# Routing products on column tiles, and a gate product on both row halves, in a two-layer gated cross-attention kernel

## The chip, the cores and the metric

The kernel is one program on one core of a Trainium2 chip. The metric is device time in microseconds of that core, from one launch that computes all sixteen examples. Lower is better.

## The reference, cut to what matters

The input is x with 16 examples of 256 tokens and 256 features. Two layers follow each other. Each has a gated attention part and a gated feed-forward part. The kernel treats them as four stages:

```python
# stage 0: attention of 16 heads over x and 77 context rows, then x += tanh(g) * (...)
# stage 1: mixture of 8 experts, two per token
logits = x @ router_w.T                       # 256 tokens x 8
probs = softmax(logits); topk_vals, topk_idx = top_k(probs, 2)
out = sum over the two: (x @ expert[topk_idx] + probs[topk_idx]) * topk_vals / (sum + 1e-6)
# stage 2: masked attention of 16 heads onto the context
# stage 3: gated linear attention, 8 heads of 64, 4 experts by token mask
low = xn @ [Wqa | Wka | Wga | Wg1a | We | Wg2a]      # 256 tokens x 256
z = low[:, ga part of 64] @ Wgb                       # 256 tokens x 512, the output gates
o = o * rsqrt(mean(o^2) + eps) * norm_w * silu(z)
x += tanh(g) * (o @ Wo)
```

The change touches two places. One is the routing of stage 1: the logits, and the ranks that say at which row of its expert's list a token goes. The other is z of stage 3, the output gates. Everything is computed in 32-bit floats.

## The kernel before, in words

**Engines and order.** TensorE, VectorE, ScalarE, GpSimd and SyncE (DMA issue) each run a program of their own. The order on an engine is the order in which the code below calls it. `pe`, `dve`, `act`, `pool` and the local `matmul` keep every instruction in that order (the helper at line 50 is the one that the profile names for most of them). An engine waits only where a semaphore makes it. A 32-bit matmul shows as two passes in the profile, so two MATMUL and two LDWEIGHTS records for each call.

**Stage 0** runs over 64 units (example b, head group g of four heads). In a unit TensorE makes the scores of this unit, the values `o` of the unit before it, and the keys and queries `qk` of the next one. The routing of examples already finished is spread over these units. In `behind_values`, `ranks` of example b-2 comes behind the values of g = 2 and `logits` of example b-1 behind those of g = 3. `logits` multiplies with the 256 tokens as the stationary operand (four matmuls of 128x128 against 8 columns). `ranks` multiplies with a triangular matrix `before` and with `ones` as the stationary operand (two matmuls, 16 columns each). Both results are copied out of PSUM by ScalarE in `copied`. The routing of the last two examples falls in stage 1. Early in stage 0, `clear_rows` fills the two lists of routed rows in DRAM with zeros from a tile `zero`, by 16 DMAs on SyncE's queue; the context's values of examples 1 and up pass through DRAM (`vctx`) on the same queue.

**Stage 3** runs over 64 slots p = 4b + m, where m is a pair of heads of example b. The main loop of `stage3_fast` writes the order of a slot out by hand; the tables `start`, `copies`, `middle`, `rest`, `late`, `behind_mask`, `by_rows` and `logs` add the steps that are made once or twice an example. In every slot TensorE makes two score products into one PSUM tile, `products(p, 0)` (`sc<-f` in the profile) and `products(p, 1)` (`sc<-q,k`). The tile `sc` has one buffer, so the second product waits until VectorE has read the first one in `masked(p, 0)` (`at<-sc,amask`). Between the two stand `route_logits`, the output gates and `second` (`gq<-low,lbk` on array rows 0 to 63 and `gz<-low,lbk` on rows 64 to 127). In slots 1 and 2 the values of the slot before (`o<-at,v`) stand there as well; in slots 0 and 3 they come behind `products(p, 1)`.

**The output gates** z of an example are 512 features by 256 tokens, four matmuls with 64 contraction rows, all on array rows 0 to 63 (`zg<-low,lbg`). `outgates(b, 0)` makes two of them in slot 0 and `outgates(b, 1)` the other two in slot 3. ScalarE reads each bank for exp(-z), VectorE copies z out of it (`zs`), ScalarE makes ln(1 + e) and exp(-ln), and GpSimd multiplies the two (`gw`). `gw` is used from slot 3 on.

**PSUM banks.** Steps that need a bank for a moment take it with `bank()`, from a pool of two buffers that are handed out in turn. An example asks for 14 of them in a fixed order. In slot 0 it is: `den` (the key softmax sums), `low`, `rt` (the expert logits of the next example, `route_logits`), `zg`. A bank is written again only when its last reader is through.

Of the kernel before, what the change touches and what calls it, by code (L numbers as in the profile page):

```python
# [10 lines left out]
F32 = mybir.dt.float32  # L11
# [15 lines left out]
def bc(ap, shape, *axes):  # L27

    for a in axes:
        ap = ap.unsqueeze(a)  # L30
    return ap.to_broadcast(list(shape))
# [42 lines left out]
def layers(ctx: ExitStack, tc: tile.TileContext, t, out, check):  # L74
# [66 lines left out]
    wo0 = load_w("wo0h" if fast else "wo0", 1024, D, w0)  # L141
    for b in range(2, B):
        load_x(b)
    rw1 = load_w("rw1", D, 8, ws1)
    ew1 = load_w("ew1", D, 2048, ws1)
    prio = const("prio", [P, 8])
    nc.sync.dma_start(out=prio, in_=t["prio"])
# [1 line left out]
    if fast:  # L149
        bv, own, pmask = (w12.tile(shape, F32, tag=n, name=n) for n, shape in (  # L150
            ("bv", [P, D]), ("own", [P, 2, 32]), ("pmask", [P, 2])))
        before, offs = (ws1.tile(shape, F32, tag=n, name=n) for n, shape in (
            ("before", [P, P]), ("offs", [P, 2, 2, 8])))

        gbo = const("gbo", [P, D])
        for n, x in (("bv", bv), ("bo", gbo), ("own", own), ("pmask", pmask), ("before", before),
                     ("offs", offs)):
            nc.sync.dma_start(out=x, in_=t[n])
    else:
        brow = w12.tile([1, 2, D], F32, tag="brow", name="brow")  # L160
        nc.sync.dma_start(out=brow, in_=t["brow"])
        bmask = w12.tile([P, 4], F32, tag="bmask", name="bmask")
        nc.sync.dma_start(out=bmask, in_=t["bmask"])
# [231 lines left out]
    class Route:  # L395
# [31 lines left out]

        def logits(self, b, bank):
            ps, xnT = bank("rt"), self.xnT.pop(b)
            for i in range(2):  # L430
                for k in range(2):
                    pe.matmul(ps[:, 8 * i:8 * i + 8], xnT[:, k, i * P:(i + 1) * P], rw1[:, k, :],
                              start=k == 0, stop=k == 1)
            self.copied(b, ps[:, :16])

        def copied(self, b, ps):
            n = ps.shape[1]
            self.ps[b] = ws1.tile([P, n], F32, tag=f"copied{n}", name="copied")
            act.copy(self.ps[b], ps)

        def exps(self, b):

            z = self.ps.pop(b)[:, :16].rearrange("p (i e) -> p i e", i=2)
            mx = st.tile([P, 2], F32, tag="rmx", name="rmx")
            dve.tensor_reduce(mx, z, AX.X, ALU.max)
            e = self.e[b] = st.tile([P, 2, 8], F32, tag="re", name="re")
            dve.tensor_tensor(e, z, bc(mx, [P, 2, 8], 2), ALU.subtract)
            act.activation(e, e, AF.Exp)
# [58 lines left out]
        def ranks(self, b, bank):  # L507
            hs, h1, h2 = self.hs[b]
            ps = bank("rank")
            pe.matmul(ps[:, :16], before, hs[:, 0].rearrange("p i e -> p (i e)"), start=True, stop=True)  # L510
            pe.matmul(ps[:, 16:32], ones, hs[:, 1].rearrange("p i e -> p (i e)"), start=True, stop=True)
            self.copied(b, ps[:, :32])

        def place(self, b):

            (_, h1, h2), ps, count = self.hs.pop(b), self.ps.pop(b), check["rows"][:, b // 8]
            base = st.tile([P, 2, 2, 8], F32, tag="base", name="base")
            at = st.tile([P, 2, 2, 2, 8], F32, tag="at", name="at")
            row = st.tile([P, 2, 2, 2], F32, tag="row", name="row")
            n = st.tile([P, 2, 8], F32, tag="nth", name="nth")  # L520
            dve.tensor_tensor(n, ps[:, :16].rearrange("p (i e) -> p i e", i=2), bc(count, [P, 2, 8], 1), ALU.add)
            dve.tensor_tensor(count, count, ps[:, 24:32], ALU.add)
            dve.tensor_tensor(n[:, 1, :], n[:, 1, :], ps[:, 16:24], ALU.add)
            dve.tensor_tensor(base[:, 0], n, offs[:, 0], ALU.add)

            dve.scalar_tensor_tensor(base[:, 1], n, ROWS - 1.0, offs[:, 1], ALU.min, ALU.add)
            for k, h in enumerate((h1, h2)):
                dve.tensor_tensor(at[:, :, :, k], base, bc(h, [P, 2, 2, 8], 1), ALU.mult)
            dve.tensor_reduce(row, at, AX.X, ALU.add)
            dve.tensor_copy(self.pos[:, b], row)  # L530
# [22 lines left out]
        return rows[e * n:e * n + ROWS].rearrange("(p n) d -> p n d", p=P)  # L553

    def clear_rows():
        zero = ws1.tile([P, D], F32, tag="zero", name="zero")
        nc.gpsimd.memset(zero, 0.0)
        n = ROWS // P
        for rows in route.rows:
            for e in range(8):  # L560
                nc.sync.dma_start(out=by_expert(rows, e),
                                  in_=bc(zero, [P, n, D], 1))

    def stage0_fast():
        with ExitStack() as sx:
# [339 lines left out]
    def stage1():  # L905
        with ExitStack() as sx:
# [7 lines left out]
            def route(b):  # L914
# [3 lines left out]
                ps = bank("rt")  # L918
                for i in range(2):
                    for k in range(2):  # L920
                        nc.tensor.matmul(ps[:, 8 * i:8 * i + 8], xnT[:, k, i * P:(i + 1) * P], rw1[:, k, :],
                                         start=k == 0, stop=k == 1)
                shape = [P, 2, 8]
                pr = softmax_last(st, "pr", ps[:, :16].rearrange("p (i e) -> p i e", i=2), shape)
# [692 lines left out]
    def stage3_fast(early_bank):  # L1617

        with ExitStack() as sx:
# [7 lines left out]
            def bank(name):  # L1627
                return pss.tile([P, 512], F32, tag="ps", name=name) if pss else early_bank(name)
# [11 lines left out]
            halves = w1.tile([P, P], F32, tag="halves", name="halves")  # L1640
            nc.sync.dma_start(out=halves, in_=t["halves"])

            lbg2 = w1.tile([64, 512], F32, tag="lbg2", name="lbg2")
            nc.sync.dma_start(out=lbg2, in_=t["lbg"][64:P, :])
            low2 = w1.tile([64, P], F32, tag="low2", name="low2")
            wo = w1.tile([P, 4, D], F32, tag="wo", name="wo")

            hots = [w1.tile([P, 2, 4], F32, tag=f"hot{n}", name=f"hot{n}") for n in range(2)]

            xn, xnT, low, lg, hT, em, am = {}, {}, {}, {}, {}, {}, {}  # L1650
            v, gw, u_, oT = {}, {}, {}, {}


# [32 lines left out]
            def lows(b):  # L1686

                low[b] = of(b).tile([P, 2, S], F32, tag="low", name="low")
                ps = bank("low")
                for c in range(2):  # L1690
                    for k in range(2):
                        matmul(ps[:, c * S:(c + 1) * S], la[:, k, c * P:(c + 1) * P], xnT[b][:, k, :],
                                         start=k == 0, stop=k == 1)
                dve3.tensor_copy(low[b][:, 0, :], ps[:, :S])
                dve3.tensor_scalar(low[b][:, 1, :], ps[:, S:], vec[:, V_ONE:V_ONE + 1], None, ALU.add)
                if b > 0:
                    for r in range(0, 64, 32):
                        dve3.tensor_scalar(low2[r:r + 32, :], ps[64 + r:96 + r, S + P:],
                                           vec[64 + r:96 + r, V_ONE:V_ONE + 1], None, ALU.add)
# [91 lines left out]
                        matmul(ps, xnT[b][:, k, tokens(i)], wv3[:, k, :], start=k == 0, stop=k == 1)  # L1791
                    act3.copy(v[b][:, i, :], ps)

            def outgates(b, i):

                if i == 0:
                    gw[b] = w2.tile([P, 4, S], F32, tag="gw", name="gw")
                ps = bank("zg")
                for m in range(2):
                    matmul(ps[:, m * S:(m + 1) * S], lbg[0:64, (2 * i + m) * P:(2 * i + m + 1) * P],  # L1800
                           low[b][0:64, 1, :], start=True, stop=True)
                e = w2.tile([P, 512], F32, tag="eg", name="eg")
                act3.activation(e, ps, AF.Exp, scale=-1.0)
                z_[b, i] = ps, e

            def outgates_end(b, i):
                ps, e = z_.pop((b, i))
                zs = w2.tile([P, 512], F32, tag="zs", name="zs")
                dve3.tensor_copy(zs, ps)
                act3.activation(e, e, AF.Ln, bias=1.0)  # L1810
                act3.activation(e, e, AF.Exp, scale=-1.0)
                pool3.tensor_tensor(gw[b][:, 2 * i:2 * i + 2, :].rearrange("p m s -> p (m s)"), zs, e, ALU.mult)


            def place(p):
# [168 lines left out]
            def warm():  # L1984

                ps = bank("warm")
                for _ in range(2):
# [7 lines left out]
            rest = {0: [(bias, 2)], 1: [(route, 1)], 2: [(steepest, 1, 0), (stats, 2)], 3: [(steepest, 1, 1), (turn_ahead, 2)]}  # L1995
            late = {1: [(scaled, -1, 1)], 2: [(project, -1)], 3: [(vals, 1)]}
            behind_mask = {0: [(route_logits, 1)]}
            by_rows = {0: [(outgates, 0, 0)], 1: [(gates_end, 1)], 3: [(outgates, 0, 1)]}
            logs = {0: [(route_sums, 1), (outgates_end, 0, 0)], 1: [(gate_logs, 1, 0)], 2: [(gate_logs, 1, 1), (norm_ahead, 2)],
                    3: [(outgates_end, 0, 1)]}  # L2000

            def run(steps, p):
                for f, d, *a in steps.get(p % 4, ()):
# [136 lines left out]
def _arrays(i):  # L2140
# [4 lines left out]
    def cols(v):  # L2145
# [32 lines left out]
        "x": f["x"], "ctx": f["ctx_1024"], "fside": f["fside_BxSxS2_0"], "mask": f["mask_BxSxS2_ik1"], "vec": vec,  # L2178
        "wkv0": f["L0_xattn_Wkv"], "wq0": f["L0_xattn_Wq"], "wo0": f["L0_xattn_Wo"],
        "wo0h": f["L0_xattn_Wo"].reshape(4, 4, 2, 32, D).transpose(0, 2, 1, 3, 4).reshape(1024, D),  # L2180
        "rw1": f["L0_ffn_router_w"].T, "ew1": f["L0_ffn_expert_weights"].transpose(1, 0, 2).reshape(D, 2048),
        "prio": np.broadcast_to(np.arange(8, 0, -1, dtype=np.float32), (P, 8)),
        "wq2": f["L1_xattn_wq_k"], "wk2": f["L1_xattn_wk_k"], "wv2": f["L1_xattn_wv_k"], "wo2": f["L1_xattn_wo_k"],
        "brow": np.stack([f["L1_xattn_wv_b"], f["L1_xattn_wo_b"]])[None], "bmask": bmask.astype(np.float32),
        "la": la, "lbk": lbk, "lbg": lbg, "we3": f["L1_ffn_We"],
        "wq3": f["L1_ffn_Wq"], "wk3": f["L1_ffn_Wk"], "wv3": f["L1_ffn_Wv"], "wo3": f["L1_ffn_Wo"],
        "before": (s < u) * np.float32(1),
        "offs": np.broadcast_to(np.float32([ALL_ROWS, ROWS]).reshape(2, 1, 1) * np.arange(8, dtype=np.float32), (P, 2, 2, 8)), "smask": smask, "halves": halves.astype(np.float32),
        "dmask": dmask.astype(np.float32), "amask": amask.astype(np.float32),
    }  # L2190
# [16 lines left out]
```

## Time and profile before

| | us |
|---|---|
| median of three runs (lowest, highest) | 1860.68 (1860.09, 1863.35) |
| the profiled execution, its own time | 1860.41 |
| span of its instructions | 1858.6 |
| stage 0 and 1 and 2 up to the first `kq` of stage 3 | 1233.9 |
| one example of stage 3 (slots 3, 0, 1, 2), TensorE busy in it | 38.14, 38.14 |
| the same, VectorE, ScalarE, GpSimd busy | 32.03, 19.23, 17.78 |

The profiled execution lies 0.3 us below the median of the runs, so sums can be made against either. Its span is 1.8 us shorter than its time. A row of the timeline reads: start, busy time, engine, line, operation, output tile <- input tiles, shape and count, and in brackets how long the engine had been idle and what released it. MATMUL and PE are TensorE's products, PEld its weight loads, DVE is VectorE, ACT ScalarE, POOL GpSimd.

### The profile page before, as it was taken

The page shows a single profiled execution, that of the slowest core. Times are in us where ns is not written, and L with a number is a line of the kernel's source. Part 1 is how long each engine was busy: PE and PEld are TensorE (multiplying, and loading weights), DVE is VectorE, ACT ScalarE, POOL GpSimd, SP SyncE. Part 2 cuts the span into 40 slices and gives each one's busy share as a digit, 9 for nine tenths or more (in the row PEclk, how much of TensorE's full clock was granted, in tenths as well). Part 3 has the DMA queues.
Part 4 walks back from the last instruction along what each step waited for, and adds up shares of the span by engine and source line. Part 5 has one row for each costly group of instructions (what it writes and reads, how often), then busy time and mean ns, then how long its engine had stood idle before and what let it go on. Part 6 is the DMA issues. An engine that isn't in the chain of part 4 may idle for free.

```text
span 1858.6 us, 34765 instructions
## 1 busy us (share of the span) xinstructions
PE 1833.0 (99%) x13678; PEld 1270.8 (68%) x13678; DVE 1231.4 (66%) x2903; ACT 863.9 (46%) x1804; POOL 1016.0 (55%) x1001
## 2 busy tenths in 40 slices
PE   8999999999999999999999999999999999999997
PEld 5666666666766667666777766667777777777775
DVE  3345656556655656555465388878888888888874
ACT  4433344343443434434343487845544545454542
POOL 4654767567666576656634767314444444444443
PEclk9999999999999999999999999999999999999999
DMA  9500010000010000000068933100000000000000
GB/s 322 204 3 20 18 32 15 25 16 22 24 37 7 29 20 10 28 24 19 10 213 249 250 50 48 18 1 1 12 7 7 7 12 7 7 7 7 13 7 14
DMA packets 56902, 84.62 MB, mean 46 GB/s; under 512 B 10467, under 2 KB 44371, under 8 KB 56217
## 3 DMA queue, kind: packets, MB, share of 16 engines
q1 hardware_dynamic: 44441, 65.52, 10.7%
q0 software_dynamic: 12288, 16.79, 4.5%
q8 instruction: 110, 1.80, 0.4%
q14 instruction: 63, 0.52, 0.1%
HBM read 44.00 MB, written 38.29 MB: 44 GB/s over the span
## 4 chain that ended last, share of the span: by engine, by line
PE 94%; DVE 2%; ACT 1%; POOL 1%; issue 1%; DMA 0%; SPq 0%; POOLq 0%; DVEq 0%; ACTq 0%
PE o L50 14%; PE qk L50 13%; PE sc L50 11%; PE v L50 9%; PE proj L50 7%; PE kq L1635 7%; PE sc L1635 5%; PE gq L1635 3%; PE ex L50 3%; PE v L1635 3%; PE proj L1635 3%; PE o L1635 3%; PE gz L1635 2%; PE low L1635 1%; PE ms L1635 1%; PE q L50 1%
## 5 line engine op out<-in xcount | busy, mean ns | idle before, releaser
L50 POOL TENSOR_SCALAR rs<-mv 128x2 f32<-128x2 f32 (+2 forms) x85 | 16.2, 191 | 395.4 <-DVE mv L50 393.2
L50 DVE RECIPROCAL rd<-o 128x256 f32<-128x256 f32 x64 | 112.4, 1756 | 162.6 <-PE o L50 162.6
L50 ACT ACTIVATE e<-sc 128x1024 f32<-128x1024 f32 (+1 forms) x192 | 181.5, 1015 | 18.5 <-PE sc L50 18.5
L50 PE MATMUL sc<-qk 64*128 64x256 f32 (+1 forms) x1536 | 183.1, 384 | 0.5 <-DVE qk L50 0.5
L50 PE MATMUL o<-e,v 128*32 128x256 f32 (+1 forms) x3072 | 177.9, 379 | 0.0
L50 PEld LDWEIGHTS sc<-qk 64*128 64x128 f32 (+1 forms) x1536 | 132.1, 172 | 55.0 <-issue 26.8
L50 POOL TENSOR_TENSOR esum<-esum,es 128x512 f32<-128x512 f32 x128 | 163.2, 1275 | 10.0
L50 PE MATMUL qk<-kvT,wkv 128*128 128x333 f32 x512 | 164.3, 443 | 0.0
L50 POOL TENSOR_TENSOR es<-e 128x1024 f32<-128x1024 f32 x64 | 151.2, 2363 | 13.7 <-ACT e L50 10.6
L50 POOL TENSOR_TENSOR at<-at,at 128x768 f32<-128x768 f32 x63 | 114.0, 1809 | 74.5 <-DVE at L50 73.6
L50 ACT ACTIVATE qk<-qk 128x256 f32<-128x256 f32 x128 | 48.9, 382 | 227.1 <-PE qk L50 227.1
L50 POOL TENSOR_TENSOR es<-es,e 77x1024 f32<-77x1024 f32 x64 | 150.3, 2348 | 5.0
L50 PEld LDWEIGHTS o<-e,v 128*32 128x32 f32 (+1 forms) x3072 | 99.8, 110 | 66.4
L50 DVE COPY qk<-qk 128x333 f32<-128x333 f32 x128 | 64.6, 505 | 106.8 <-ACT qk L50 104.9
L50 PE MATMUL qk<-kvT,wq 128*128 128x256 f32 x512 | 134.4, 385 | 0.0
L50 POOL DMA_INDIRECT x<-rows_out,pos x64 | 100.9, 1577 | 34.7 <-issue 17.2
L50 PEld LDWEIGHTS qk<-kvT,wkv 128*128 128x128 f32 x512 | 97.2, 190 | 30.0
L50 PEld LDWEIGHTS qk<-kvT,wq 128*128 128x128 f32 x512 | 94.4, 189 | 33.7 <-issue 13.7
L50 PE MATMUL proj<-wo0h,oT 128*128 128x256 f32 x512 | 113.5, 380 | 0.0
L50 PE MATMUL v<-wkv,kvT 128*128 128x512 f32 x256 | 113.0, 594 | 0.0
L50 POOL TENSOR_TENSOR gw<-zs,eg 128x512 f32<-128x512 f32 x32 | 40.7, 1273 | 120.5 <-ACT eg L50 115.8
L50 PEld LDWEIGHTS proj<-wo0h,oT 128*128 128x128 f32 x512 | 96.0, 190 | 13.3 <-issue 0.8
(261 smaller groups left out, 4124.4 us busy)
## 6 DMA issues: line engine op xcount, KB each, us to landing
rows<-zero SPq DMA_DIRECT2D x16, 640.0 KB
xin<-rows SPq DMA_DIRECT2D x16, 640.0 KB
rows_out<-y SPq DMA_DIRECT2D x16, 384.0 KB
v<-vctx SPq DMA_DIRECT2D x15, 308.0 KB
x<-in_x_dram SPq DMA_DIRECT2D x16, 256.0 KB
rows_out<-y SPq DMA_DIRECT2D x16, 256.0 KB
out_dram<-x SPq DMA_DIRECT2D x15, 256.0 KB
wkv<-in_wkv_dram SPq DMA_DIRECT2D x2, 1024.0 KB
```

Source lines behind the costliest of these rows:

```text
L50: x = getattr(self.engine, name)(*a, **k)
L1635: tc.keep_in_program_order(nc.tensor.matmul(*a, **k))
```

## The change

In the routing, the operands of the two products change sides. The router weights (padded from 8 to 32 columns with zeros) and the choice matrix `hs` (32 columns) become the stationary operands, and the tokens stream past them, 64 columns to a matmul, in four 32-column tiles of the array. The results come out transposed, and VectorE turns them in 32x32 blocks out of PSUM (`turned`), where ScalarE copied before. `before` grows by 32 columns of ones. The tile `zero` shrinks to 128 columns, so the zeroing DMAs read pieces of 512 bytes in place of 1,024.

In stage 3, all four output-gate products of an example stand in slot 0. Two run on array rows 0 to 63, two on rows 64 to 127; for that the rows `low[0:64]` are copied to partitions 64 to 127 (`lowd`) by a DMA right after they are made, and `lbg` is loaded there a second time. Each row half writes a bank of its own. ScalarE makes the copy `zs` in place of VectorE, directly behind exp. `outgates_end` of the second half moves from slot 3 to slot 1.

```diff
-    rw1 = load_w("rw1", D, 8, ws1)
+    rw1 = load_w("rw1", D, 32, ws1)
...
         def logits(self, b, bank):
-            for i in range(2):
-                for k in range(2):
-                    pe.matmul(ps[:, 8 * i:8 * i + 8], xnT[:, k, i * P:(i + 1) * P], rw1[:, k, :],
+            for k in range(2):
+                for q in range(4):
+                    pe.matmul(ps[32 * q:32 * q + 32, :64], rw1[:, k, :],
+                              xnT[:, k, :].rearrange("p (i q t) -> p i q t", i=2, q=4)[:, :, q, :],
                               start=k == 0, stop=k == 1)
-            self.copied(b, ps[:, :16])
+            self.turned(b, ps)
...
+        def turned(self, b, ps):
+            self.ps[b] = ws1.tile([P, 2, 32], F32, tag="turned", name="turned")
+            dve.transpose(self.ps[b].rearrange("p n e -> p (n e)"), ps[:, :64])
...
         def ranks(self, b, bank):
-            pe.matmul(ps[:, :16], before, hs[:, 0].rearrange("p i e -> p (i e)"), start=True, stop=True)
-            pe.matmul(ps[:, 16:32], ones, hs[:, 1].rearrange("p i e -> p (i e)"), start=True, stop=True)
-            self.copied(b, ps[:, :32])
+            for q in range(4):
+                pe.matmul(ps[32 * q:32 * q + 32, :64], hs.rearrange("p w i e -> p (w i e)"),
+                          before[:, q:5:4 - q, :], start=True, stop=True)
+            self.turned(b, ps)
...
     def clear_rows():
-        zero = ws1.tile([P, D], F32, tag="zero", name="zero")
+        zero = ws1.tile([P, P], F32, tag="zero", name="zero")
-                nc.sync.dma_start(out=by_expert(rows, e),
-                                  in_=bc(zero, [P, n, D], 1))
+                nc.sync.dma_start(out=by_expert(rows, e).rearrange("p n (x d) -> p (n x) d", d=P),
+                                  in_=bc(zero, [P, 2 * n, P], 1))
...
+            lbg2 = w1.tile([P, 512], F32, tag="lbg2", name="lbg2")
+            nc.sync.dma_start(out=lbg2[:64], in_=t["lbg"][64:P, :])
+            nc.sync.dma_start(out=lbg2[64:], in_=t["lbg"][:64, :])
...
             def lows(b):
+                lowd[b] = of(b).tile([P, S], F32, tag="lowd", name="lowd")
+                nc.sync.dma_start(out=lowd[b][64:], in_=low[b][:64, 1, :])
...
-            def outgates(b, i):
-                if i == 0:
-                    gw[b] = w2.tile([P, 4, S], F32, tag="gw", name="gw")
-                ps = bank("zg")
-                for m in range(2):
-                    matmul(ps[:, m * S:(m + 1) * S], lbg[0:64, (2 * i + m) * P:(2 * i + m + 1) * P],
-                           low[b][0:64, 1, :], start=True, stop=True)
-                e = w2.tile([P, 512], F32, tag="eg", name="eg")
-                act3.activation(e, ps, AF.Exp, scale=-1.0)
-                z_[b, i] = ps, e
+            def outgates(b):
+                gw[b] = w2.tile([P, 4, S], F32, tag="gw", name="gw")
+                two = [bank("zg"), bank("zg")]
+                for i in range(2):
+                    for h, (w, x) in enumerate(((lbg[0:64], low[b][0:64, 1, :]), (lbg2[64:], lowd[b][64:]))):
+                        m = 2 * i + h
+                        matmul(two[h][:, i * S:(i + 1) * S], w[:, m * P:(m + 1) * P], x, start=True, stop=True)
+                for h, ps in enumerate(two):
+                    e, zs = (w2.tile([P, 512], F32, tag=n, name=n) for n in ("eg", "zs"))
+                    act3.activation(e, ps, AF.Exp, scale=-1.0)
+                    act3.copy(zs, ps)
+                    z_[b, h] = zs, e
...
-                zs = w2.tile([P, 512], F32, tag="zs", name="zs")
-                dve3.tensor_copy(zs, ps)
...
-            by_rows = {0: [(outgates, 0, 0)], 1: [(gates_end, 1)], 3: [(outgates, 0, 1)]}
-            logs = {0: [(route_sums, 1), (outgates_end, 0, 0)], 1: [(gate_logs, 1, 0)], 2: [(gate_logs, 1, 1), (norm_ahead, 2)],
-                    3: [(outgates_end, 0, 1)]}
+            by_rows = {0: [(outgates, 0)], 1: [(gates_end, 1)]}
+            logs = {0: [(route_sums, 1), (outgates_end, 0, 0)], 1: [(outgates_end, 0, 1), (gate_logs, 1, 0)],
+                    2: [(gate_logs, 1, 1), (norm_ahead, 2)]}
```

More of the change, by code (lines that the diff above doesn't have):

```diff
@@ L152, in layers @@
         before, offs = (ws1.tile(shape, F32, tag=n, name=n) for n, shape in (
-            ("before", [P, P]), ("offs", [P, 2, 2, 8])))
+            ("before", [P, 5, 32]), ("offs", [P, 2, 2, 8])))
         gbo = const("gbo", [P, D])
@@ L429, in logits @@
             ps, xnT = bank("rt"), self.xnT.pop(b)
-            for i in range(2):
-                for k in range(2):
-                    pe.matmul(ps[:, 8 * i:8 * i + 8], xnT[:, k, i * P:(i + 1) * P], rw1[:, k, :],
+            for k in range(2):
+                for q in range(4):
+                    pe.matmul(ps[32 * q:32 * q + 32, :64], rw1[:, k, :],
+                              xnT[:, k, :].rearrange("p (i q t) -> p i q t", i=2, q=4)[:, :, q, :],
                               start=k == 0, stop=k == 1)
-            self.copied(b, ps[:, :16])
[L436 to L439, printed above, removed]
+            self.turned(b, ps)
+        def turned(self, b, ps):
+            self.ps[b] = ws1.tile([P, 2, 32], F32, tag="turned", name="turned")
+            dve.transpose(self.ps[b].rearrange("p n e -> p (n e)"), ps[:, :64])
         def exps(self, b):
-            z = self.ps.pop(b)[:, :16].rearrange("p (i e) -> p i e", i=2)
+            z = self.ps.pop(b)[:, :, :8]
             mx = st.tile([P, 2], F32, tag="rmx", name="rmx")
@@ L520, in place @@
             n = st.tile([P, 2, 8], F32, tag="nth", name="nth")
-            dve.tensor_tensor(n, ps[:, :16].rearrange("p (i e) -> p i e", i=2), bc(count, [P, 2, 8], 1), ALU.add)
-            dve.tensor_tensor(count, count, ps[:, 24:32], ALU.add)
-            dve.tensor_tensor(n[:, 1, :], n[:, 1, :], ps[:, 16:24], ALU.add)
+            dve.tensor_tensor(n, ps[:, 0, :16].rearrange("p (i e) -> p i e", i=2), bc(count, [P, 2, 8], 1), ALU.add)
+            dve.tensor_tensor(count, count, ps[:, 1, 24:32], ALU.add)
+            dve.tensor_tensor(n[:, 1, :], n[:, 1, :], ps[:, 1, 16:24], ALU.add)
             dve.tensor_tensor(base[:, 0], n, offs[:, 0], ALU.add)
@@ L920, in route @@
                     for k in range(2):
-                        nc.tensor.matmul(ps[:, 8 * i:8 * i + 8], xnT[:, k, i * P:(i + 1) * P], rw1[:, k, :],
+                        nc.tensor.matmul(ps[:, 8 * i:8 * i + 8], xnT[:, k, i * P:(i + 1) * P], rw1[:, k, :8],
                                          start=k == 0, stop=k == 1)
@@ L1641, in stage3_fast @@
             nc.sync.dma_start(out=halves, in_=t["halves"])
-            lbg2 = w1.tile([64, 512], F32, tag="lbg2", name="lbg2")
-            nc.sync.dma_start(out=lbg2, in_=t["lbg"][64:P, :])
+            lbg2 = w1.tile([P, 512], F32, tag="lbg2", name="lbg2")
+            nc.sync.dma_start(out=lbg2[:64], in_=t["lbg"][64:P, :])
+            nc.sync.dma_start(out=lbg2[64:], in_=t["lbg"][:64, :])
             low2 = w1.tile([64, P], F32, tag="low2", name="low2")
@@ L1648, in stage3_fast @@
             hots = [w1.tile([P, 2, 4], F32, tag=f"hot{n}", name=f"hot{n}") for n in range(2)]
-            xn, xnT, low, lg, hT, em, am = {}, {}, {}, {}, {}, {}, {}
+            xn, xnT, low, lg, hT, em, am, lowd = {}, {}, {}, {}, {}, {}, {}, {}
             v, gw, u_, oT = {}, {}, {}, {}
@@ L1792, in vals, with outgates_end @@
                     act3.copy(v[b][:, i, :], ps)
-            def outgates(b, i):
-                if i == 0:
-                    gw[b] = w2.tile([P, 4, S], F32, tag="gw", name="gw")
-                ps = bank("zg")
-                for m in range(2):
-                    matmul(ps[:, m * S:(m + 1) * S], lbg[0:64, (2 * i + m) * P:(2 * i + m + 1) * P],
-                           low[b][0:64, 1, :], start=True, stop=True)
-                e = w2.tile([P, 512], F32, tag="eg", name="eg")
-                act3.activation(e, ps, AF.Exp, scale=-1.0)
-                z_[b, i] = ps, e
-            def outgates_end(b, i):
-                ps, e = z_.pop((b, i))
-                zs = w2.tile([P, 512], F32, tag="zs", name="zs")
-                dve3.tensor_copy(zs, ps)
+            def outgates(b):
[10 more added lines that the diff above has]
+                    z_[b, h] = zs, e
+            def outgates_end(b, h):
+                zs, e = z_.pop((b, h))
                 act3.activation(e, e, AF.Ln, bias=1.0)
                 act3.activation(e, e, AF.Exp, scale=-1.0)
-                pool3.tensor_tensor(gw[b][:, 2 * i:2 * i + 2, :].rearrange("p m s -> p (m s)"), zs, e, ALU.mult)
+                pool3.tensor_tensor(gw[b][:, h::2, :], *(x.rearrange("p (m s) -> p m s", m=2) for x in (zs, e)), ALU.mult)
             def place(p):
@@ L1997, in stage3_fast @@
             behind_mask = {0: [(route_logits, 1)]}
-            by_rows = {0: [(outgates, 0, 0)], 1: [(gates_end, 1)], 3: [(outgates, 0, 1)]}
-            logs = {0: [(route_sums, 1), (outgates_end, 0, 0)], 1: [(gate_logs, 1, 0)], 2: [(gate_logs, 1, 1), (norm_ahead, 2)],
-                    3: [(outgates_end, 0, 1)]}
+            by_rows = {0: [(outgates, 0)], 1: [(gates_end, 1)]}
+            logs = {0: [(route_sums, 1), (outgates_end, 0, 0)], 1: [(outgates_end, 0, 1), (gate_logs, 1, 0)], 2: [(gate_logs, 1, 1), (norm_ahead, 2)]}
             def run(steps, p):
@@ L2180, in _arrays @@
         "wo0h": f["L0_xattn_Wo"].reshape(4, 4, 2, 32, D).transpose(0, 2, 1, 3, 4).reshape(1024, D),
-        "rw1": f["L0_ffn_router_w"].T, "ew1": f["L0_ffn_expert_weights"].transpose(1, 0, 2).reshape(D, 2048),
+        "rw1": np.concatenate([f["L0_ffn_router_w"].T, z((D, 24), np.float32)], axis=1), "ew1": f["L0_ffn_expert_weights"].transpose(1, 0, 2).reshape(D, 2048),
         "prio": np.broadcast_to(np.arange(8, 0, -1, dtype=np.float32), (P, 8)),
@@ L2186, in _arrays @@
         "wq3": f["L1_ffn_Wq"], "wk3": f["L1_ffn_Wk"], "wv3": f["L1_ffn_Wv"], "wo3": f["L1_ffn_Wo"],
-        "before": (s < u) * np.float32(1),
+        "before": np.concatenate([(s < u) * np.float32(1), np.ones((P, 32), np.float32)], axis=1).reshape(P, 5, 32),
         "offs": np.broadcast_to(np.float32([ALL_ROWS, ROWS]).reshape(2, 1, 1) * np.arange(8, dtype=np.float32), (P, 2, 2, 8)), "smask": smask, "halves": halves.astype(np.float32),
```

## The prediction

> **What bounds the kernel now.** I read the page's engine shares first, then the chain that ended last, then the waits, and last the timeline around the places that change.
>
> ```profile
> PE 1833.0 (99%) x13678; PEld 1270.8 (68%) x13678; DVE 1231.4 (66%) x2903; ACT 863.9 (46%) x1804; POOL 1016.0 (55%) x1001
> ...
> PE 94%; DVE 2%; ACT 1%; POOL 1%; issue 1%; DMA 0%; SPq 0%; POOLq 0%; DVEq 0%; ACTq 0%
> ```
>
> TensorE is busy 99% of the span and carries 94% of the chain. The waits list has no long wait of PE. So a microsecond taken from TensorE's stream is worth a microsecond, but only if what follows it is not waiting for another engine. That must be read place by place. First the routing (example near 125 us), and the same for the ranks:
>
> ```profile
> 124.82 1.48 PE L50 MATMUL o<-e,v 128*32 128x256 f32 x24
> 126.23 1.06 PE L50 MATMUL rt<-rw,rxnT 128*128 128x8 f32 x8
> 127.14 1.11 PE L50 MATMUL qk<-kvT,wq 128*128 128x256 f32 x4
> ...
> 165.01 0.40 PE L50 MATMUL rank<-hs,before 128*128 128x16 f32 x2
> 165.26 0.37 PE L50 MATMUL rank<-hs,ones 128*128 128x16 f32 x2
> 165.48 1.96 PE L50 MATMUL v<-wkv,ctxT 128*128 128x512 f32 x4
> ```
>
> No idle is shown: `rt` holds TensorE from 126.23 to 127.14, 0.91 us, and `rank` from 165.01 to 165.48, 0.47 us. Now slot 0 of stage 3:
>
> ```profile
> 1510.19 0.92 PE L1635 MATMUL sc<-f 64*128 64x256 f32 x8
> 1510.95 0.28 PE L1638 MATMUL rt<-ident,low 64*128 64x64 f32 x2
> 1511.03 0.91 PE L1635 MATMUL zg<-low,lbg 64*128 64x256 f32 x3
> 1511.23 0.96 DVE L50 TENSOR_TENSOR at<-sc,amask 128x768 f32<-128x768 f32 x1 [0.26 <-PE rt L1638]
> 1511.99 0.59 PE L1635 MATMUL gq<-low,lbk 64*128 64x256 f32 x2
> 1512.11 0.15 DVE L50 TENSOR_REDUCE emx<-rt 128x2 f32<-128x8 f32 x1
> 1512.30 0.17 DVE L50 TENSOR_TENSOR e<-rt,emx 128x8 f32<-128x8 f32 x1
> 1512.34 0.92 PE L1635 MATMUL sc<-q,k 64*128 64x256 f32 x8
> ```
>
> And slot 3, VectorE and TensorE:
>
> ```profile
> 1499.45 2.84 DVE L50 STREAM_TRANSPOSE xnT<-xn 32x128 f32<-32x128 f32 x9
> 1502.32 0.96 DVE L50 TENSOR_TENSOR at<-sc,amask 128x768 f32<-128x768 f32 x1
> ...
> 1501.22 0.92 PE L1635 MATMUL sc<-f 64*128 64x256 f32 x8
> 1501.98 0.81 PE L1635 MATMUL zg<-low,lbg 64*128 64x256 f32 x3
> 1502.84 0.59 PE L1635 MATMUL gq<-low,lbk 64*128 64x256 f32 x2
> 1503.42 0.92 PE L1635 MATMUL sc<-q,k 64*128 64x256 f32 x8
> ```
>
> In both slots `sc<-q,k` starts 0.14 to 0.15 us after `at` ends (1511.23 + 0.96 = 1512.19; 1502.32 + 0.96 = 1503.28). It could not start sooner, whatever TensorE does. The `zg`, `gq` and `gz` passes just fill that wait.
>
> **The change part by part: routing.** A pass of 256 columns spaces the next by 0.216 us (slot 3: zg starts 1501.98, third one 1502.41); the eight `rt` passes of 8 columns space by 0.111, set by their 128-column weight loads. After the change there are 16 passes of 64 columns in four rounds of four column tiles. That four tiles do run side by side is in `o<-e,v`: four passes start within 0.02 us, the next four 0.22 later, one 256-column spacing. No row has 64 columns on 32-column tiles, so a round is bounded: below by the two `rt<-ident,low` passes of 64 columns, which start 0.055 apart, above by 0.11, today's weight-bound spacing. I take 0.085. `rt` becomes 0.34 (0.22 to 0.44), saving 0.57 (0.47 to 0.69). `rank`, eight passes, two rounds, becomes 0.17 (0.11 to 0.22), saving 0.30 (0.25 to 0.36). The switch between full array and tiles costs 0.09 (the first pass behind `o` starts 0.307 after the last, not 0.216); it stood ahead of `rt` and now stands behind it, so it counts once as before. Fourteen examples in stage 0: 14 x 0.87 = 12.2. The last two lie in stage 1 between full-array products and pay a second switch: about 0.3 for both. Sum **-12.5 us (-10 to -15)**.
>
> On VectorE 32 transposes of 128x64 are added; the nearest rows are `dens<-den` 128x256 at 0.44 and `xnT` 32x128 at 0.30, so about 0.2 each, 6 us in all. They stand between `oT` and the first `qk` copy, and that copy was idle 1.04 us before it, waiting for ACT. Queued behind the transpose's wait for `rt` are only copies of products that TensorE makes later. If that cover were gone, 6 us would be lost. ScalarE loses 32 copies of 0.17 to 0.19, worth nothing at 46% busy.
>
> Zeroing: 10.5 MB in packets of 1,024 bytes at 46 ns each, issued 37.1 to 63.0 us at the engines' pace. 512-byte packets take 27 ns in this trace, so the stretch grows by 2 x 27 / 46 = 1.17, by 4.5 us. Behind it on SyncE's queue waits `vctx`, whose read for example 1 is issued at 70.1 and needed by `o<-e,v` at 89.1. Cost nothing, with some 14 us of cover left. If a small packet cost the full 46 ns, the queue would be 26 us late and TensorE would stand about 10 us; the measured 27 speaks against it.
>
> **Slot 3.** Out go four `zg` passes. On rows 0 to 63 there stood zg 4 + gq 2 = 6 passes, 1.3 us; now gq and gz side by side, 0.43. But `sc<-q,k` still waits for `at`, and `at` starts where it did: VectorE's transposes end at 1502.29, and it is busy from 1532.4 on in the next example's copy of this stretch without a gap. TensorE becomes idle for 0.86 us. Saving 0 to 0.06 an example. Here I weigh the Trainium skill's TensorEngine Tiling (Array Packing), Theoretical Speedup: contraction of 64 or less is up to twice as fast on two row tiles. By that rule four passes of 0.216 go, 16 x 0.86 = 13.8 us, and the sum would be 1834. By the rows it is under 1 us, since the time saved lies under VectorE's 0.96. I take the rows.
>
> **Slot 0.** Bank order is den, low, rt, zg, zg over two buffers: the first zg follows `low`, the second follows `rt`. So the first product on rows 64 to 127 waits until VectorE has read `rt`, and these two reads stand behind `at`: they end at 1512.30 + 0.17 = 1512.47. TensorE makes two zg passes from 1511.03 and then stands from about 1511.57 to 1512.58 (0.11 from VectorE's end to the load, as 1512.19 to 1512.31 now). Queued behind it in order are the other zg, gq, gz and `sc<-q,k`. Then rows 64 to 127 have zg 4 and gz 2 passes: 0.32 for the first (1511.03 to 1511.35 today) and 5 x 0.216 = 1.40. `sc<-q,k` starts at 1513.98, where its first load today has the same start-up at 1512.34, steady from 1512.43. **Loss 1.45 to 1.55** in each of 15 examples (the last asks for no `rt`): 22.5, less slot 3's 0.06 x 15: **+21.5 us (17 to 24)**. The same page's Gotcha 1 (row tiles write different banks) is why a second bank is asked for at all.
>
> Does the period absorb it? No: TensorE is busy 38.14 of 38.14 us, and nothing else waits less if it is late. ScalarE gets two copies of 0.585 (`rxnT<-rtr`, the same shape) in slot 0. Its queue there: two exp, two copies, one exp, two `eg`, one square, 4.6 us from 1513.35, ends 1517.9; `z` of slot 1 needs it at 1518.6. 0.7 us of cover; beyond it each microsecond delays `sc<-f` of slot 1. VectorE loses 32 x 0.68 and still waits for TensorE. GpSimd's first `gw` ends at 1518.6 and `at` behind it at 1520.4, needed at 1521.3. The `lowd` copies, 16 of 64 KB on SyncE's queue, are issued four slots ahead (38 us); an output store behind them comes 13 us later. Nothing.
>
> **Sum.** 1860.4 - 12.5 + 21.5 = 1869.4, against the profiled 1860.41, 0.3 below the median; I say **1869**. About 0.2%, 3.7 us, is what a measurement can tell from no change.
>
> **The rivals.** A (0.68) is the above, own range 1861 to 1877.
>
> B (0.10), faster: the second bank is free when asked for. Then zg is done in slot 0's existing 1.3 us on both halves, and only routing counts: 1848. It decides at 1511.46, the end of the first zg pair: readers done by then cost nothing. For it: slot 0's filler has room. Against: VectorE starts to read `rt` at 1512.11, behind `at`.
>
> C (0.14): TensorE passes the waiting product and runs zg, gq on rows 0 to 63 and gz meanwhile. For it: gz starts at 1502.42, ahead of gq at 1502.84, though it is issued behind. The skill's TensorE: Matmul & The Clock Gate, The mechanism, says products keep strict order and only loads are pulled ahead; that row differs. Against C stands the end of the kernel, where ready zg passes did not go past `sc<-f`:
>
> ```profile
> 1835.01 0.92 PE L1635 MATMUL sc<-f 64*128 64x256 f32 x8 [0.45 <-DVE at L50]
> 1835.77 1.03 PE L1635 MATMUL zg<-low,lbg 64*128 64x256 f32 x4
> ```
>
> Four zg passes still lie behind the wait: loss 0.32 + 3 x 0.216 from 1512.58, 1513.55 - 1512.43 = 1.1, x 15 = 17: 1864. By strict order (the rule) it is A's 1869.
>
> D (0.08): zeroing at 46 ns a packet, +10 on A: 1879.
>
> **Numbers.** Range 1856 to 1884: A, C and D with the routing's bounds; B is left out. Faster: B and a little of C, 0.13; same: 0.09; slower: 0.78.
>
> **What would show it.** Right: stage 3's example grows from 38.14 to about 39.6; in slot 0 `zg<-lowd` is released by DVE e about 1 us late, in slot 3 `sc<-q,k` by DVE at behind an idle TensorE; `rt` takes 0.3 to 0.4 and `rank` under 0.25. Wrong: an example of 38.1 or less, `zg<-lowd` starting with `zg<-low`, or a late `v<-vctx` near 89 us.

## The result and the profile after

The changed kernel takes 1872.23 us, the median of four runs (1871.66 to 1875.32), against 1860.76 for the kernel before, run on the same chip: the ratio is 1.0059, with a 95% interval of 1.0046 to 1.0073. It is slower, by 11.5 us. The profiled execution of the changed kernel spans 1869.9 us, 11.3 more than the 1858.6 of before.

The head of the page after, engine shares and the chain that ended last:

```profile
PE 1815.8 (97%) x13870; PEld 1253.7 (67%) x13870; DVE 1236.5 (66%) x2903; ACT 875.3 (47%) x1804; POOL 1017.2 (54%) x1001
...
PE 77%; DVE 10%; POOL 7%; issue 3%; ACT 2%; DMA 1%; POOLq 0%; SPq 0%; DVEq 0%; ACTq 0%
```

TensorE works 17.2 us less than before (1833.0), as both parts of the edit intended, yet its share falls from 99% to 97%. Its part of the chain falls from 94% to 77%; VectorE's rises from 2% to 10% and GpSimd's from 1% to 7%. So TensorE's saved time has become waiting. The waits list of TensorE says for what (engine, tile, releaser; us in total, times, longest). Before, it had 1.6 us in four waits of `sc` for `at`, and none of `zg` or for `es`:

```profile
PE sc L1637 <- DVE at L50: 14.9, 18, 1.2
PE zg L1637 <- issue: 12.5, 15, 0.8
...
PE o L50 <- POOL es L50: 2.0, 8, 0.4
```

The first two belong to stage 3, where they come once in each of fifteen examples (and in a few slots at its beginning and end). The third belongs to stage 0. I take them one by one, in the order of the kernel.

**Routing.** The timeline after, example near 125 us, and its neighbour for the ranks:

```profile
124.23 2.35 PE L50 MATMUL o<-e,v 128*32 128x256 f32 x40
126.40 0.41 PE L50 MATMUL rt<-rxnT,rw 128*32 128x64 f32 x16
126.74 1.13 PE L50 MATMUL qk<-kvT,wq 128*128 128x256 f32 x4
...
164.51 0.30 PE L50 MATMUL rank<-before,hs 128*32 128x64 f32 x8
164.74 3.70 PE L50 MATMUL v<-wkv,ctxT 128*128 128x512 f32 x8
```

From the start of the last pass of `o` to the start of the first pass of `qk` TensorE took 1.22 us before (125.92 to 127.14) and takes 0.53 now (126.20 to 126.74). For the ranks it was 0.77 and is 0.42. All fourteen examples of stage 0 show the same two savings, 0.69 and 0.35. The four rounds of four column tiles start at 126.40, 126.46, 126.51 and 126.57, about 0.055 apart; a row of `rt` in the timeline is longer (0.41), because a pass of 64 columns keeps its record open for 0.22 us while the next ones are already running.

**Slot 0 of stage 3**, after, from the first score product to the second:

```profile
1511.42 0.92 PE L1637 MATMUL sc<-f 64*128 64x256 f32 x8
...
1512.18 0.28 PE L1640 MATMUL rt<-ident,low 64*128 64x64 f32 x2
1512.26 0.70 PE L1637 MATMUL zg<-low,lbg 64*128 64x256 f32 x2
1512.46 0.96 DVE L50 TENSOR_TENSOR at<-sc,amask 128x768 f32<-128x768 f32 x1 [0.26 <-PE rt L1640]
1513.34 0.16 DVE L50 TENSOR_REDUCE emx<-rt 128x2 f32<-128x8 f32 x1
1513.53 0.17 DVE L50 TENSOR_TENSOR e<-rt,emx 128x8 f32<-128x8 f32 x1
...
1513.79 0.45 PE L1637 MATMUL zg<-lowd,lbg 64*128 64x256 f32 x1 [0.84 <-issue]
...
1514.95 0.38 PE L1637 MATMUL gz<-low,lbk 64*128 64x256 f32 x1
1514.98 0.99 PE L1637 MATMUL sc<-q,k 64*128 64x256 f32 x7
```

VectorE ends its last read of `rt` at 1513.53 + 0.17 = 1513.70. The first product on the second bank starts at 1513.79, after an idle TensorE of 0.84 us. The profile says only "issue" there, so the releaser has to be found by its end, which is VectorE's `e<-rt`: in all fifteen examples the product starts 0.10 us behind that end. TensorE makes the first `kq` products once a slot, so the time from one `kq` to the next measures a slot. The interval that holds this stretch grew from 8.34 to 9.83 us, +1.49.

**Slot 3**, after:

```profile
1498.48 5.04 DVE L50 STREAM_TRANSPOSE xnT<-xn 32x128 f32<-32x128 f32 x16
...
1502.43 0.92 PE L1637 MATMUL sc<-f 64*128 64x256 f32 x8
...
1503.41 0.38 PE L1637 MATMUL gq<-low,lbk 64*128 64x256 f32 x1
1503.42 0.38 PE L1637 MATMUL gz<-low,lbk 64*128 64x256 f32 x1
1503.55 0.96 DVE L50 TENSOR_TENSOR at<-sc,amask 128x768 f32<-128x768 f32 x1
...
1504.65 0.92 PE L1637 MATMUL sc<-q,k 64*128 64x256 f32 x8 [0.86 <-DVE at L50]
```

`at` starts as soon as VectorE's transposes end (1498.48 + 5.04 = 1503.52), ends at 1504.51, and `sc<-q,k` follows 0.14 later, exactly as before. The four passes that were taken out left a hole of 0.86 us. The interval that holds it is 11.55 us after and 11.54 before: the saving is zero.

Over the span, counted from the first product of each execution: the last `rt` pass stands 12.3 us earlier than before, the first `kq` of stage 3 9.4 us earlier, and the 63 intervals between the `kq` groups add up to 612.25 against 590.34 us, +21.9.

### The profile page after: what moved, and what is told of

It is laid out like the page before. It is cut to its first block, busy times and chain, and to the rows that moved or that the text cites. A ratio compares the mean times of both kernels' runs of the same rounds, so it can differ in the third digit from the quotient of the medians.

```text
span 1869.9 us, 35183 instructions
## 1 busy us (share of the span) xinstructions
PE 1815.8 (97%) x13870; PEld 1253.7 (67%) x13870; DVE 1236.5 (66%) x2903; ACT 875.3 (47%) x1804; POOL 1017.2 (54%) x1001
## 4 chain that ended last, share of the span: by engine, by line
PE 77%; DVE 10%; POOL 7%; issue 3%; ACT 2%; DMA 1%; POOLq 0%; SPq 0%; DVEq 0%; ACTq 0%
PE o L50 11%; PE qk L50 11%; PE v L50 8%; PE sc L50 8%; PE proj L50 7%; PE kq L1637 5%; PE sc L1637 5%; POOL es L50 4%; DVE xnT L50 3%; PE proj L1637 3%; PE o L1637 3%; PE gq L1637 3%; PE ex L50 3%; DVE at L50 2%; POOL rs L50 2%
## 5 line engine op out<-in xcount | busy, mean ns | idle before, releaser
L50 ACT ACTIVATE ee<-gq 128x256 f32<-128x256 f32 x128 | 42.0, 383 | 136.4 <-PE gq L1637 136.4
```

The costliest lines, as they stand in the source:

```text
L50: x = getattr(self.engine, name)(*a, **k)
```

## The experiments

All kernels of one group below ran on one chip together with the kernel before; ratios are to those runs.

**The two halves of the change alone.** `e1_routing_only` is the kernel before with the routing hunks and the small zero tile, `e2_gates_only` the kernel before with the stage 3 hunks; both are cuts of the diff that is shown above.

> The kernel before with the routing on column tiles alone (and its zeroing), stage 3 as it was. The trace of after shows 12.45 us won up to the end of the routing, and then 2.4 to 3 us lost again ahead of stage 3. If those losses come with the routing, the span falls by 9.5 to 10.5 us: about 1850.5 us. Rival: the losses (a mask load that moved on SyncE's queue, a stretch of half clock near 1211 us) belong to that one execution or to the stage 3 edit: then 12.5 us, 1848.

> The kernel before with the stage 3 edit alone. Bank theory: slot 0 of stage 3 grows by 1.49 us in 15 examples, the last example is 0.35 shorter: +22.0, so 1882.7 us, and sc<-q,k of slot 3 stands 0.86 us behind at. Rival (the edits disturb each other, part of the 22 us is a consequence of the routing): less than +20.

Routing alone took 1849.45 us, ratio 0.9936 (0.9919 to 0.9952), 13.1 below the 1862.58 of before in that group. Its last `rt` pass stands 12.5 us earlier than before, its first `kq` 10.6 us. The interval of the ratio, 9 to 15 us, holds both expectations, so the time alone does not decide between them. The trace does. About 2 us were lost ahead of stage 3 here too, but the lead over before was still 12.3 us at 1216.5 us; then TensorE ran at half clock (column 0.57 of this view, explained with `e8_before_again` below), and 1.7 us went:

```profile
1216.00:1220.00 4.00, 4.00 (x8) 1.56 (x6) 2.66 (x12) 1.50 (x5) 0.00 (x0) 0.57 0.00 0
```

The kernel before shows the same loss in its second profile, so it does not come with the routing: the rival expectation was the better one.

Stage 3's edit alone took 1883.64, ratio 1.0114 (1.0097 to 1.0131), 21.1 above before, with the same intervals as in the changed kernel (9.83 and 11.55 us). The halves add up, -13.1 + 21.1 = +8.0, and the whole is +11.5, with about 3 us of uncertainty on each. No disturbance of one by the other shows, in the times or in the intervals.

**The bank.** Is the loss in slot 0 the wait for `rt`'s bank, or the work that was added there? In `e3_rt_later` no instruction is taken away; `route_logits` is asked for one slot later, so `rt` takes its bank behind the two `zg`.

```diff
-            copies = {2: [(turned_hot, 1)]}
+            copies = {1: [(route_logits, 1)], 2: [(turned_hot, 1)]}
-            rest = {0: [(bias, 2)], 1: [(route, 1)], ...
+            rest = {0: [(bias, 2)], 1: [(route_sums, 1), (route, 1)], ...
-            behind_mask = {0: [(route_logits, 1)]}
+            behind_mask = {}
-            logs = {0: [(route_sums, 1), (outgates_end, 0, 0)], ...
+            logs = {0: [(outgates_end, 0, 0)], ...
```

> The changed kernel with one difference: route_logits is asked for one slot later, behind the next slot's mask, so that the two zg banks follow den and low, and rt takes a bank that the first zg left. Every instruction is kept. Bank theory: the 0.84 us stall goes, zg, gq and gz are done inside the wait for at, slot 0 falls from 9.83 to about 8.34 us: -22 us against the changed kernel, about 1850. Rival (the 1.49 us are the added ScalarE copies, or TensorE's time for passes on both halves): the time stays at 1872.

It took 1853.64 us, ratio 0.9951 (0.9935 to 0.9968). The changed kernel's ratio was 1.0059, so 0.0108 of 1861 us, 20 us, came back with no instruction taken away. The edit moves `rt` and its two readers out of the stretch together with the order of banks; `zg` does not read `rt`, so only the bank ties the waiting product to the end of that last reader, 0.10 us ahead of it in every example. Slot 0's interval is 8.60 us. That is 0.26 above the 8.34 that I expected, 15 x 0.26 = 3.9 us in all, and the timeline of the next kernel shows where they are: the `rt` transposes no longer stand inside the wait for `at` but on TensorE's path. The ScalarE copies and the `lowd` DMAs are all still there, and no interval shows a cost of theirs.

**The hole in slot 3.** `e4_rt_later_o_inside` is the same with `o<-at,v` of the slot before moved into the hole:

```diff
-                inside = p % 4 in (1, 2) and p + 1 < last
+                inside = p % 4 in (1, 2, 3) and p + 1 < last
```

> As the one with route_logits later, and o<-at,v is put between the products in slot 3 as well (it was in slots 1 and 2), into the 0.86 us in which TensorE stands there. If the idle time can be used, slot 3 falls by 0.8 us in 15 examples: 12 us more, about 1838 us, below both kernels. Rival (at of the step before is not ready, or f and q of the next step come later and become the bound): no more than 1850, or slower.

It took 1839.41 us (1839.00 to 1841.55), ratio 0.9880 (0.9864 to 0.9897): 22 us faster than before and 33 faster than the changed kernel. Slot 0 in its timeline:

```profile
1494.48 0.92 PE L1637 MATMUL sc<-f 64*128 64x256 f32 x8
...
1495.23 0.38 PE L1637 MATMUL zg<-low,lbg 64*128 64x256 f32 x1
1495.32 0.48 PE L1637 MATMUL zg<-lowd,lbg 64*128 64x256 f32 x1
...
1495.52 0.96 DVE L50 TENSOR_TENSOR at<-sc,amask 128x768 f32<-128x768 f32 x1 [0.26 <-PE sc L1637]
...
1496.50 0.38 PE L1637 MATMUL gz<-low,lbk 64*128 64x256 f32 x1
1496.62 0.92 PE L1637 MATMUL sc<-q,k 64*128 64x256 f32 x8
...
1497.47 0.87 PE L1637 MATMUL o<-at,v 128*64 128x256 f32 x8
...
1498.28 0.33 PE L1640 MATMUL rt<-ident,low 64*128 64x64 f32 x2
1498.54 1.13 PE L1637 MATMUL kq<-xnT,wk 128*128 128x256 f32 x4
```

Now `zg<-lowd` starts 0.09 us behind `zg<-low`, all of `zg`, `gq` and `gz` have started by 1496.50, as VectorE's `at` ends (1495.52 + 0.96 = 1496.48), and `sc<-q,k` starts 0.14 after that end. `rt` takes 0.26 us between `o` and `kq` (1498.28 to 1498.54). Slot 3:

```profile
1523.90 0.92 PE L1637 MATMUL sc<-f 64*128 64x256 f32 x8
1524.75 0.87 PE L1637 MATMUL o<-at,v 128*64 128x256 f32 x8
1525.55 0.48 PE L1637 MATMUL gq<-low,lbk 64*128 64x256 f32 x1
...
1526.09 0.85 PE L1637 MATMUL sc<-q,k 64*128 64x256 f32 x8
```

`o` stands in the hole, no idle is shown, and the interval fell from 11.55 to 10.65 us, by 0.90. An example takes 37.51 us, against 38.13 before and 39.63 with the change.

**The hole with the stall kept.** `e5_after_o_inside` is the changed kernel with that one line of `inside` alone. In its expectation, "slot 3" is the `kq` interval of 11.55 us that holds the hole.

> The changed kernel with one difference: o<-at,v also stands between the products in slot 3. The bank stall in slot 0 stays. If the two stalls are independent, slot 3 falls from 10.15+11.55 us with slot 2 by 0.90 us, slot 0 keeps its 9.83: 13.5 us less than the changed kernel, 1859, about the time before. Rival (with the stall in slot 0 kept, another engine takes what slot 3 wins): less than 8 us won.

It took 1859.21 us, ratio 0.9989 (0.9982 to 0.9996), 13 us less than the changed kernel, as expected: 10.65 us for the interval with slot 3, 9.83 still for slot 0. The two losses are independent.

**How strictly TensorE keeps its order.** `e9_gq_gz_first` leaves banks and readers as in the changed kernel and only asks for `gq` and `gz` ahead of `zg` in slot 0:

```diff
-            by_rows = {0: [(outgates, 0)], 1: [(gates_end, 1)]}
+            by_rows, behind_second = {1: [(gates_end, 1)]}, {0: [(outgates, 0)]}
...
                     factors_second(p + 1)
+                run(behind_second, p)
```

> The changed kernel with one difference: in slot 0 the four gq and gz passes are asked for ahead of the zg products, not behind. The second zg bank is the same and comes free at the same time. If TensorE takes products strictly in order, two passes on rows 64 to 127 now lie ahead of the stall instead of behind it: slot 0 falls by 2 x 0.216 = 0.43 us, from 9.83 to 9.40, 6.5 us in all, about 1866. If TensorE passes a waiting product and runs later ready ones meanwhile, gq and gz were never behind the stall, and the time stays at 1872.

Slot 0 fell to 9.40 us, to the digit, and the time was 1865.64, ratio 1.0022 (1.0013 to 1.0030). Its timeline:

```profile
1508.61 0.38 PE L1637 MATMUL gz<-low,lbk 64*128 64x256 f32 x1
1508.77 0.38 PE L1637 MATMUL zg<-low,lbg 64*128 64x256 f32 x1
1509.73 0.45 PE L1637 MATMUL zg<-lowd,lbg 64*128 64x256 f32 x1 [0.59 <-issue]
1509.74 0.48 PE L1637 MATMUL zg<-low,lbg 64*128 64x256 f32 x1
...
1510.46 0.38 PE L1637 MATMUL zg<-lowd,lbg 64*128 64x256 f32 x1
1510.49 0.99 PE L1637 MATMUL sc<-q,k 64*128 64x256 f32 x7
```

At 1509.74 stands a `zg<-low` product on rows 0 to 63. Its bank was free and its rows were idle for 0.6 us. It did not start until the product ahead of it, on the other rows, had its bank.

**Where the routing's saving ends.** `e6_routing_no_esum` is routing alone without GpSimd's two additions a unit into `esum`; the kernel leaves out this running sum, which guards against overflow.

```diff
-                for n in range(2):
-                    pool.tensor_tensor(esum, esum, es[:, n, :], ALU.add)
```

> Routing alone, and GpSimd's 128 additions of es into esum are left out (a running sum that only guards against overflow). Theory: the routing frees 1.04 us of TensorE an example, and 2 us of it over the 14 examples go into waits of o for es, GpSimd's sums. With GpSimd relieved, the 8 waits of o for es go and the last rt stands 2 us earlier than with routing alone, 14.5 us earlier than before. Rival (the missing 2 us went elsewhere): the last rt stands where it does with routing alone, within 0.5 us.

The last `rt` pass stands 14.9 us earlier than before, 2.4 more than with routing alone, and of the eight waits for `es` one is left. The row of routing alone, then of this kernel:

```profile
PE o L50 <- POOL es L50: 1.9, 8, 0.4
```

```profile
PE o L50 <- POOL es L50: 0.4, 1, 0.4
```

The time was 1846.94, ratio 0.9925 (0.9909 to 0.9942). That interval overlaps the one of routing alone, so the 2.4 us are read from the traces, not from the times. What the routing's saving ran into in stage 0 is GpSimd's sums. In before, TensorE had no wait at all in a list of waits between 60 and 900 us.

**Zeroing.** `e7_zero_512B` is the kernel before with the small zero tile alone.

> The kernel before with the zeroing alone in packets of 512 bytes. The prediction gave the stretch 4.5 us more, hidden: vctx of the first example still lands ahead of the product that reads it, and the time is that of before within 0.2%. Rival (a small packet costs as much as a large one): the stretch is 26 us longer, TensorE waits for vctx near 89 us, +10 us.

It took 1859.87 us, ratio 0.9997 (0.9989 to 1.0006): no difference. SyncE's queue (start, time of issue) before, in this kernel, and in the changed one:

```profile
37.14 25.83 SPq L561 DMA_DIRECT2D rows<-zero  x16
```

```profile
37.89 31.04 SPq L561 DMA_DIRECT2D rows<-zero  x16
```


```profile
37.49 36.02 SPq L563 DMA_DIRECT2D rows<-zero  x16
73.60 5.46 SPq L664 DMA_DIRECT2D vctx<-vc  x3
80.47 0.28 SPq L666 DMA_DIRECT2D v<-vctx  x1
```

The three lengths are no accident of one execution: the other profiles without this edit show 25.86 and 25.89 us, and all seven with the new routing 35.94 to 36.02. Why the routing adds 5 us to what the small tile costs alone was not tried. In the changed kernel `o<-e,v`, which reads what comes back, starts at 89.39 without a wait.

**Before once more.** `e8_before_again` is the kernel before, unchanged.

> The kernel before, unchanged, profiled once more. In four of the five changed kernels TensorE ran at half clock for 3 to 5 us between 1208 and 1240 us, in the profile of before it did not. If that belongs to an execution, it may show here too, at 1215 to 1250 us; if it belongs to the change, it can not.

It does show it. The windows of the changed kernel, of this one, and of the first profile of before; the column behind the last (x...) is the clock that TensorE was granted, as a share of full speed:

```profile
1206.00:1210.00 4.00, 3.32 (x48) 1.47 (x39) 2.01 (x4) 3.86 (x7) 0.00 (x0) 1.00 0.07 16
1210.00:1214.00 4.00, 3.46 (x12) 2.35 (x16) 3.71 (x3) 1.87 (x4) 0.00 (x0) 0.60 0.02 4
```

```profile
1216.00:1220.00 4.00, 3.69 (x63) 1.88 (x54) 1.71 (x3) 3.34 (x7) 0.00 (x0) 1.00 0.00 0
1220.00:1224.00 4.00, 3.10 (x11) 2.06 (x8) 3.93 (x6) 2.82 (x4) 0.00 (x0) 0.72 0.01 2
1224.00:1228.00 4.00, 4.00 (x53) 1.90 (x55) 1.44 (x3) 0.94 (x4) 0.00 (x0) 0.85 0.00 0
```

```profile
1220.00:1224.00 4.00, 3.10 (x26) 1.99 (x28) 3.93 (x5) 2.59 (x4) 0.00 (x0) 1.00 0.00 0
```

The same eight `proj<-wo,oT` passes, behind the same idle of 0.90 us, took 1.97 us in the first profile of before, 3.46 in this second one and 3.47 in the changed kernel, where they are 0.427 us apart instead of about 0.21. From just ahead of the stretch to the first `kq`, the changed kernel and this one both fall back by 1.64 us against the first profile. So this part of the loss belongs to an execution and not to the change.

## Why the prediction was right

The forecast was 1869, range 1856 to 1884, with slower at 0.78. The measured 1872.2 lies in the range, on the side named, and in rival A's own range. Step by step:

- **Slot 0: right, in mechanism and size.** A loss of 1.45 to 1.55 was forecast in each of 15 examples; it is 1.49. The second `zg` bank follows `rt`, its readers stand behind `at`, and TensorE stands until they are through. `e3_rt_later` shows the cause and `e9_gq_gz_first` the arithmetic of passes behind the stall. The path behind the stall was a little different from the one worked out: `sc<-q,k` starts 1.20 us later against `sc<-f` than before (3.35 in place of 2.15), and the other 0.29 are lost from there to `o` (1.14 in place of 0.85).
- **Slot 3: right.** A saving of 0 to 0.06 was forecast; it is 0.00. Time taken from work that lies under a wait is not saved. `e5_after_o_inside` shows that it is there to be used.
- **The packing rule.** By the Trainium skill's TensorEngine Tiling (Array Packing), Theoretical Speedup, two row tiles would have saved 13.8 us (the estimate from its factor of two). The passes do run side by side (`zg<-low` and `zg<-lowd` 0.09 us apart in `e4_rt_later_o_inside`), so the rule holds for the products; but none of it reached the time before the hole was filled, as the rows said.
- **Rival C falls.** Strict order was the right reading, and `e9_gq_gz_first` measures it. The rule in the skill's TensorE: Matmul & The Clock Gate, The mechanism (products in strict order), holds at a wait. `gz` ahead of `gq` in the prediction's row is only a different start among products that are all ready.
- **Rival B falls**: the second bank was not free when asked for.
- **Routing: the sum right, the terms not.** I had 0.57 for `rt` and 0.30 for `rank`; they measured 0.69 and 0.35. The mis-sized term is a round of 64 columns: I took 0.085 us and it is 0.055, the bound set by `rt<-ident,low`. Fourteen examples at 1.04 would be 14.6 us. What came out at the last `rt` was 12.3, because about 2 us went into waits for GpSimd's `es`, which the prediction did not name: it had counted stage 0 as bounded by TensorE alone. Two errors cancelled, so the exact sum was luck. VectorE's transposes took 0.24 us each where I said 0.2, and were hidden.
- **Zeroing: hidden, as forecast, but mis-sized.** 4.5 us more were worked out, 5.2 were measured alone and 10.2 in the changed kernel, where `v<-vctx` was issued 10.3 us later; the second half of that growth has no explanation here. Rival D needed 26.
- **Not in the sum.** Between the last rank and the first `kq` the changed kernel loses 3.0 us. The half clock is 1.64 of them. Another 0.8 go near 970 us: VectorE waited 2.4 us for a mask load (`mk`), and TensorE's `xT` then 0.7 for VectorE. The longest such wait for `mk` is 0.4 to 1.5 us in the four profiles with the routing of before and 1.0 to 2.6 in the seven with the new one; why, was not tried. In the other direction, one interval with slot 3 near the end of the kernel is 0.35 us shorter (11.48 against 11.83). It is so with the routing alone and with stage 3's edit alone as well, and its cause was not looked for.

Together: -12.4 at the last rank, +3.0 up to stage 3, +21.9 in stage 3 make +12.5. The first product started 0.3 us later and the end behind the last product was 1.6 us shorter, in an execution each; that leaves the measured +11.3 of the spans.

## What to carry to other kernels

Where short-lived tiles share a rotating pool of banks, asking for one more bank in a place changes whose release every later product waits for; write down the order of requests and the last reader of each, and ask first for the tile that is needed first and last for the one whose reader is late. A product that is made faster between two others is worth nothing while the second waits for another engine: pair the cut with something from TensorE's own path that can be moved into the hole, and read the result from the interval around it. Here both cuts were sound, and two changes of order turned +11.5 us into -22.

## What the runs showed of the hardware

- A product that waits for its bank holds up ready products on the other row half of the array: 0.59 us in `e9_gq_gz_first`, though those rows were idle.
- Column-tile rounds of 64 columns follow each other in 0.055 us, four tiles within 0.02 us, even with a weight load for every pass. Going back to the full array costs about 0.09 us: the first `qk` pass starts 0.149 us behind the last `rt` pass, 0.094 more than a round. How much of that is the change of tiles and how much the longer weight load of `qk`, no run separates.
- In nine of the eleven profiles TensorE fell to half clock in the middle of its work, between 1209 and 1237 us (in one near 1816). From the granted clock of the windows the stretches come out at 3.4 us, in two profiles there is one of 6.8: in the second profile of before, (1 - 0.72) x 4 us x 2 + (1 - 0.85) x 4 us x 2 = 3.4. TensorE's idle just ahead of it was 0.90 us there, and the identical idle left the clock at 1.00 in the first profile of the same kernel; in `e1_routing_only` TensorE was busy for 4.00 of the 4.00 us in which the clock fell, and its records show no idle for 6.8 us ahead of that. The Trainium skill's TensorE: Matmul & The Clock Gate, What's actually happening, tells of a free-running window of about 3.4 us whose phase differs from run to run; the length agrees. That it takes idle gaps over about 3.4 us, as the same page's HAM oscillation section has it, these profiles do not bear out. Six profiles have one stretch of 3.4 us ahead of stage 3 that can be measured against the first profile of before, and each lost 1.64 to 1.70 us in it. That is a part of the 3 to 5 us by which runs of one kernel differ here; what makes a stretch come or stay away, no run shows.
